# A fused attention and LoRA layer on one core: five transfers and sums moved at the start and near the end

## The chip, the core and the metric

The kernel runs on one core of a Trainium2 chip. The core has a matrix engine (TensorE, PE in the profile, with its weight loads as PEld), a vector engine (VectorE, DVE), a scalar engine (ScalarE, ACT), a general engine (GpSimd, POOL) and SyncE (SP), which here only issues transfers. Each engine runs its own list of instructions in order and waits for semaphores of the others. The metric is the device time of one execution in microseconds. A difference of 0.3% is about what a measurement of this kernel can tell from no change; here that is 2.45 us.

## The reference, cut to what matters

`x` is 2 x 512 tokens of 512 numbers, all in float32. There are 32 query heads, 8 key and value heads and a head size of 128.

```
q, k, v = x @ Wq + bq, x @ Wk + bk, x @ Wv + bv        # per head; q and k are then turned by the rope tables
p       = softmax(causal(q k^T / sqrt(128)))           # 4 query heads share one key head
x1      = layernorm(x + (p v) @ Wo + bo)
y       = x1 @ W_base^T + b_base + sum over 4 experts of alpha_e * 2 * (x1 A_e^T) B_e^T
out     = layernorm(x1 + y)                            # alpha: softmax over the 4 active experts' router logits
```

## The kernel before

**Units, parts, slots.** One unit `u` is a key head with one of the two sequences (16 units). A unit has four parts, one for each 128 queries; part `i` of a unit looks at `i + 1` tiles of 128 keys. All 64 parts stand in a list, and each takes four slots, one for each 32 queries of its four heads. Slot `T` computes the scores of step `T` on PE (L574); the other stages of the same step follow in later slots: masked maximum on DVE and exponential on ACT one slot later (L582, L589), reciprocal after two, normalisation on ACT after three (L597), transposition in 32 x 32 blocks on DVE after four (L605, L607). When the four steps of a part are transposed, `blocks_out` writes them to DRAM (`db`, four transfers, L615), and in a later slot `blocks_in` reads them back as `pT` with keys on the partitions (L626). From slot 4p + 12 on, one key tile in each slot, `weigh` multiplies `pT` by the values (L633). The scores have two PSUM buffers: the product of slot T can start only when the exponential of slot T - 2 has been taken.

The order is written out by hand. `slot(T)` issues, in this order, the projections of later units, the output products (`wo_products`), the scores, the weighting, the copies and the softmax stages; `put(T, f)` adds work at the end of a slot. The last two units are 14 and 15; their parts are 56 to 63, in the order of keys 1, 2, 3, 4 and then 3, 4, 1, 2 tiles. The parts that matter here are 58 (three tiles), 59 (four), 60 (three) and 61 (four).

**Strassen-like products.** The query projection and the output projection use seven products in place of eight, so sums of blocks are made ahead: `x_sums` on DVE (L441, four for each sequence), `w_sums` and `ctx_sums` on POOL (L449 to L452). Each result is added to `x_sb` from PSUM by `wo_adds` on DVE (L697). In most pairs of parts the add stands one slot after its product. For the last two pairs, 28 and 29, it stands in the same slot, and pair 28 begins in slot 247.

**The beginning.** SP loads four token tiles of x with the first key weights between them, then the query weights. PE transposes each tile, DVE or ACT copies it to `xT` (L288), and PE multiplies it by the key weights (L412). Then come the sums of x on DVE and the sums of query weights on POOL, which the seven products of the first query heads need.

**The end.** `W_base` has been transposed in blocks through DRAM (`wb_rows`) during the middle. From slot 237 on (`T_PROJ`) the memory of the projections is free, and `wb_sb` (1 MB in two transfers, L1231) lies in it. ACT copies it to `wbT` (L1226), which the first feed-forward products read in slot 251 (L805). Meanwhile DVE takes the statistics of the first four token tiles (L730), POOL does the Newton steps of their inverse roots (L754 to L757), and DVE centres them (L760).

**What orders one engine behind another here.** SP issues its transfers in program order: `pT` of a part waits there for all four `db` writes of that part to land. DVE's add waits for PE's product and holds everything that stands behind it on DVE.

Of the kernel before, what the change touches and what calls it, by code (L numbers as in the profile page):

```python
# [15 lines left out]
P = 128  # L16
# [3 lines left out]
D = 128  # L20
# [9 lines left out]
def postln_layer_kernel(  # L30
# [33 lines left out]
    nc = tc.nc  # L64
    B, S, HID = x.shape
    NT = B * S // P
    TPB = S // P
# [6 lines left out]
    NU = G * B  # L74
# [71 lines left out]
    wos = {}  # L146
    wvs = {}

    def load_k(g):
        wk_g = wts.tile([P, KC, D], F32, tag="wk_g", name=f"wk_{g}")  # L150
        nc.sync.dma_start(out=wk_g, in_=Wk[:, ts(g, D)].rearrange("(c p) n -> p c n", p=P))
        wqk["k", g] = wk_g

    def load_q(n, k):
# [15 lines left out]
    def load_x(t, n):  # L170
        nc.sync.dma_start(
            out=x_sb[:, t : t + n, :], in_=xf[t * P : (t + n) * P, :].rearrange("(t p) n -> p t n", p=P))


    for n in range(2):
# [6 lines left out]
        out=tri, in_=tri, pattern=[[-BLK, QB], [-1, BLK]], compare_op=ALU.is_ge,  # L182
# [7 lines left out]
    for z in zt:  # L190
        nc.gpsimd.memset(z, 0.0)

    for t in range(2):
        load_x(t, 1)
    load_k(0)
    for t in range(2, TPB):
        load_x(t, 1)
    load_q(0, 0)
    bqk = setup.tile([NBIAS, D], F32, name="bqk")
# [26 lines left out]

    ar_act = setup.tile([P, HID], F32, name="ar_act")
    lp_rep = setup.tile([P, P], F32, name="lp_rep")
    for part in (ar_act, lp_rep):
        nc.gpsimd.memset(part, 0.0)  # L230
    rb_act = setup.tile([EA, 1], F32, name="rb_act")
    pr_act = setup.tile([EA, 1], F32, name="pr_act")
    b_act = setup.tile([P, EA, BJ * RK], F32, name="b_act")
# [120 lines left out]
    parts = [(u, i) for u in range(NU) for i in ((2, 3, 0, 1) if u == NU - 1 else range(TPB))]  # L354
# [50 lines left out]
    def k_tile(u, t, c):  # L405

        g, b = unit(u)
        key = "k", u
        if t == c == 0:
            psq[key] = ps_k.tile([P, S], F32, tag="k", name="pp")  # L410
            in_psum.add(key)
        nc.tensor.matmul(  # L412
            psq[key][:, ts(t, P)], lhsT=wqk["k", g][:, c, :], rhs=xT[:, c, ts(b * TPB + t, P)],
            start=(t == c == 0), stop=(c == KC - 1), skip_group_check=True)
# [22 lines left out]
    def x_sums(b, step, engine=nc.vector):  # L437
        b11, b12, b21, b22 = (
            xT[:, CH * k : CH * (k + 1), b * S + a * TH : b * S + (a + 1) * TH] for k in range(2) for a in range(2))
        t1, t2, t3, t4 = (xs[:, b, k] for k in range(4))  # L440
        engine.tensor_tensor(  # L441
            *((t1, b12, b11), (t2, b22, t1), (t3, b22, b12), (t4, b21, t2))[step], ALU.subtract)

    def w_block(n, k, head, c_half):
        return wqk["q", n, k][:, CH * c_half : CH * (c_half + 1), ts(head, D)]

    def strassen_sums(engine, a11, a12, a21, a22, s1, s2, s4):

        engine.tensor_tensor(s1, a21, a22, ALU.add)  # L449
        engine.tensor_tensor(s2, s1, a11, ALU.subtract)  # L450
        engine.tensor_tensor(s4, a12, s2, ALU.subtract)
        engine.tensor_tensor(a21, a11, a21, ALU.subtract)  # L452

    def w_sums(n, k):
        w = ws[n, k] = proj.tile([P, 3, CH, D], F32, tag=f"ws{k}", name=f"ws_{n}_{k}")
        strassen_sums(
            nc.gpsimd, *(w_block(n, k, h, c) for h in range(2) for c in range(2)), *(w[:, m] for m in range(3)))
# [8 lines left out]
    def q_products(u, k, step):  # L466
        n, b = set_of(u), unit(u)[1]
        key = u, k
        w = ws[n, k]
        x1, x2 = (xT[:, CH * c : CH * (c + 1), ts(b, S)] for c in range(2))  # L470
        if step == 1:
            halves[key] = {"qx": ps_q.tile([P, TH], F32, tag="qx", name="qx")}
            product(halves[key]["qx"], w_block(n, k, 0, 0), x1[:, :, :TH], True)
        elif step == 2:
            halves[key]["qy"] = ps_q.tile([P, TH], F32, tag="qy", name="qy")
            product(halves[key]["qy"], w_block(n, k, 0, 1), x2[:, :, :TH], True)
        elif step == 6:
            product(halves[key]["qx"], w[:, 1], xs[:, b, 1], False)
        elif step == 5:
            product(halves[key]["qy"], w[:, 0], xs[:, b, 0], True)  # L480
        elif step == 7:
            product(halves[key]["qx"], w_block(n, k, 1, 0), xs[:, b, 2], False)
        elif step == 4:
            product(halves[key]["qx"], w_block(n, k, 1, 1), xs[:, b, 3], False)
        else:
            product(halves[key]["qy"], w[:, 2], x2[:, :, TH:], False)
# [6 lines left out]
    def q_copy(u, k, name):  # L493
        if name == "p1":
            psq["q", u, 2 * k] = proj.tile([P, S], F32, tag="raw0", name="q0", bufs=2)
        elif name == "u3":
            psq["q", u, 2 * k + 1] = proj.tile([P, S], F32, tag="raw1", name="q1")
        nc.scalar.copy(q_half(u, k, name), halves[u, k]["qx"])  # L498

    def q_sum(u, k, name):  # L500
        into = q_half(u, k, name)
        nc.vector.tensor_tensor(into, halves[u, k]["qy"], into, ALU.add)
# [106 lines left out]
    def blocks_out(p):  # L609

        i = parts[p][1]
        z, last = zt[i % 2], TPB - 2 + i % 2
        db[p] = dram.tile([QB, BLK, R, (i + 1) * P], F32, tag=f"db{i}", name=f"db_{p}")
        for r in range(R):
            nc.sync.dma_start(  # L615
                out=db[p][:, :, r, :].rearrange("q t x -> t q x"),
                in_=z[ts(r, BLK), :, last - i : last + 1].rearrange("t q j n s -> t q (j n s)"))

    def blocks_in(p):

        i = parts[p][1]
        pT[p] = work.tile([P, R, (TPB - 1 + i % 2) * P], F32, tag=f"pT{i % 2}", name=f"pT_{p}", bufs=1)

        for lo, hi in ((0, 1), (1, i + 1)) if i > 1 and parts[p][0] >= NU - 2 else ((0, i + 1),):
            cols = slice(lo * P, hi * P)
            nc.sync.dma_start(out=pT[p][:, :, cols], in_=db[p][:, :, :, cols].rearrange("q t r x -> (q t) r x"))  # L626

# [274 lines left out]
    def put(slot, f):  # L902
        extra.setdefault(slot, []).append(f)
# [95 lines left out]
        for step in (0, 1, 2, 3, 4, 6, 7):  # L999
            wo_at[8 * k + LAG_WO + step] = (k, (step,))  # L1000
    LAST_PAIRS = LAST + LAG_WO + 2
    for n, steps in enumerate(((0,), (1,), (2,), (3,), (4,), (6, 7))):
        wo_at[LAST_PAIRS + n] = (WO_PAIRS - 2, steps)
    for n, steps in enumerate(((0, 1), (2, 3), (4, 7), (6,))):
        wo_at[LAST_PAIRS + 6 + n] = (WO_PAIRS - 1, steps)
# [111 lines left out]
    for t in range(TPB - 2, TPB):  # L1117
        for c in range(KC):
            k_tile(0, t, c)
    for n in range(4):  # L1120
        x_sums(0, n)
    for k in range(2):
        w_sums(0, k)


    def v_first(t):
# [3 lines left out]
    for k in range(2):  # L1130
        for step in (1, 2, 6, 5, 7):
            q_products(0, k, step)
            if step == 1:
                q_copy(0, k, "p1")
            elif step == 2:
                q_sum(0, k, "p1")
                if k:
                    q_rope(0, 0, 2)
                    for part in range(3):
                        k_rope(0, part)  # L1140
                    for n in range(3):
                        x_sums(1, n, nc.gpsimd)
            elif step == 6:
                q_copy(0, k, "u2")
            elif step == 7:
                q_copy(0, k, "u3")
        q_sum(0, k, "u3")
        if k == 0:
            expert_rows()
        v_first(2 * k)  # L1150
        q_products(0, k, 4)
        q_copy(0, k, "c21")
        if k:
            prior_weights(0)
            q_rope(0, 3, 0)
        q_products(0, k, 3)
        q_sum(0, k, "u2")
        v_first(2 * k + 1)
        if k == 0:
            for t in range(TPB, NT):  # L1160
                transpose_token_tile(
                    xT[:, :, ts(t, P)], x_sb[:, t, :], *spare[(2, 3, 0, 3)[t - TPB]], nc.scalar.copy)
        for part in range(k, 3):
            q_rope(0, 2 * k + 1, part)
        if k:
            x_sums(1, 3, nc.gpsimd)
            for part in range(3):
                put(T_BEGIN + part, lambda part=part: q_rope(0, 2, part))
        else:
            for part in range(2):  # L1170
                q_rope(0, 0, part)
# [8 lines left out]
    T_PROJ = T_END - 19  # L1180
# [44 lines left out]
    def transposed_base(c):  # L1225
        nc.scalar.copy(  # L1226
            wbT[:, :, c // 2, ts(c % 2, P)].rearrange("p k (a s) -> p k a s", s=BLK),
            wb_sb[:, c].rearrange("p a k s -> p k a s"))

    for n in range(2):  # L1230
        put(T_PROJ + 9, lambda n=n: nc.sync.dma_start(  # L1231
            out=wb_sb[:, 2 * n : 2 * n + 2].rearrange("p c a k s -> p c a (k s)"),
            in_=wb_rows[:, :, 2 * n : 2 * n + 2].rearrange("q t c a x -> (q t) c a x")))
    for c in range(OC):
        put(T_PROJ + (12, 12, 13, 13)[c], lambda c=c: transposed_base(c))
    put(A - 5, lambda: f0[0].norm1.newton(0, 2))
    for k, f in enumerate(f0):
        put(A + (-7, -6, 0, 0)[k], f.stats)
# [160 lines left out]
```

## Time and profile before

| what | us |
|---|---|
| median of 3 runs (lowest, highest) | 815.27 (814.25, 816.87) |
| the profiled execution's own time | 816.12 |
| its span, first to last instruction | 814.3 |
| PE busy in it | 803.9 |
| DVE, ACT, POOL busy in it | 615.6, 382.6, 349.3 |
| granted TensorE clock | 0.999 of full speed |

The span is 1.8 us shorter than the profiled execution's own time; that execution is 0.85 us above the median of the runs. In the timeline, a row gives the start, the duration, the engine, the line, the operation with its output and inputs, and in brackets the idle time of the engine before it with what ended that. The rows of PE overlap by some tenths, because matmuls are pipelined and their ends are modelled.

### The profile page before, as it was taken

Reading aid. Unit: us, or ns where it says so; the run is one execution under the profiler, and the core shown is the slowest. Engines: PE = TensorE matmul, PEld = TensorE weight load, DVE = VectorE, ACT = ScalarE, POOL = GpSimd, SP = SyncE. Lnnn points to the kernel's source line nnn. Section 1 sums busy time; section 2 is a strip of 40 time slices with the busy share of each in tenths; the row PEclk is TensorE's granted clock in tenths of the full one; section 3 lists DMA queues with packets and bytes.
Section 4 is the critical chain, followed back from the end, with each engine's and each line's share of the span. In section 5 each row is a group of like instructions: output and inputs, shape, how many; then the busy total and the mean of one; then the engine's idle time right before and its main releaser. Section 6 shows DMA issues by size and latency. Waiting matters only on the chain.

```text
span 814.3 us, 11458 instructions
## 1 busy us (share of the span) xinstructions
PE 803.9 (99%) x3457; PEld 611.7 (75%) x3457; DVE 615.6 (76%) x1994; ACT 382.6 (47%) x1072; POOL 349.3 (43%) x404
## 2 busy tenths in 40 slices
PE   8999999999999999999999999999999999999997
PEld 7887777777777778777777878777777877657565
DVE  4778877687879886787868777787888689985455
ACT  2355454444545454545535454444545444654243
POOL 8666645421444445322443245343564433461033
PEclk9999999999999999999999999999999999999999
DMA  9025737355465647364554537355453725577311
GB/s 308 17 72 143 219 81 203 93 130 155 145 182 130 191 103 221 91 170 140 141 168 130 171 82 236 110 155 181 130 155 91 232 66 152 177 226 230 121 39 65
DMA packets 91376, 119.15 MB, mean 146 GB/s; under 512 B 6957, under 2 KB 71325, under 8 KB 89522
## 3 DMA queue, kind: packets, MB, share of 16 engines
q1 hardware_dynamic: 90642, 118.12, 50.4%
q8 instruction: 27, 0.44, 0.2%
q0 software_dynamic: 448, 0.14, 0.1%
q14 instruction: 35, 0.29, 0.1%
q10 hardware_dynamic: 224, 0.16, 0.1%
HBM read 72.78 MB, written 45.61 MB: 145 GB/s over the span
## 4 chain that ended last, share of the span: by engine, by line
PE 94%; POOL 2%; DVE 1%; DMA 1%; ACT 1%; issue 0%; DVEq 0%; POOLq 0%
PE pc L633 16%; PE sc L574 14%; PE qx L462 14%; PE wx L462 12%; PE qy L462 10%; PE wy L462 9%; PE kx L462 4%; PE vx L540 4%; PE py L805 3%; PE pv L360 3%; PE po L711 2%; PE pp L377 1%; DMA wb_sb<-wb_rows 1%; PE py L846 1%; PE tp L287 0%; PE ph L863 0%
## 5 line engine op out<-in xcount | busy, mean ns | idle before, releaser
L589 ACT ACTIVATE p<-sc,nmax 128x288 f32<-128x288 f32 (+15 forms) x256 | 124.2, 485 | 199.7 <-DVE nmax L582 181.2
L582 DVE CUSTOM_DVE_ANT_0 sc<-sc,maskw 128x288 f32<-128x288 f32 (+15 forms) x256 | 114.1, 446 | 131.7 <-PE sc L574 130.2
L633 PE MATMUL pc<-pT,v 128*128 128x512 f32 x320 | 165.6, 600 | 1.7 <-DMA pT<-db 1.6
L398 POOL TENSOR_TENSOR qT<-q,t 128x512 f32<-128x512 f32 x64 | 88.1, 1377 | 176.4 <-DVE q L397 165.3
L574 PE MATMUL sc<-kT,qT 128*128 128x160 f32 (+15 forms) x512 | 161.9, 398 | 0.9 <-ACT p L589 0.8
L597 ACT ACTIVATE p<-p,den 128x288 f32<-128x288 f32 (+15 forms) x256 | 133.2, 520 | 3.7 <-DVE den L593 3.7
L574 PEld LDWEIGHTS sc<-kT,qT 128*128 128x128 f32 x512 | 95.9, 190 | 20.1 <-issue 5.3
L449 POOL TENSOR_TENSOR cs<-ctxT 128x256 f32<-128x256 f32 x30 | 23.9, 796 | 168.6 <-PE wy L462 105.5
L640 ACT ACTIVATE ctxT<-pc,bqkT 128x512 f32<-128x512 f32 x64 | 44.0, 688 | 109.1 <-PE pc L633 108.5
L605 DVE STREAM_TRANSPOSE zt<-p 128x128 f32<-128x128 f32 (+2 forms) x192 | 81.6, 425 | 0.0
L633 PEld LDWEIGHTS pc<-pT,v 128*128 128x128 f32 x320 | 57.0, 190 | 21.2 <-issue 5.5
L498 ACT COPY q<-qx 128x256 f32<-128x256 f32 x128 | 47.4, 370 | 52.5 <-PE qx L462 52.3
L462 PE MATMUL qx<-xs,wq 128*128 128x256 f32 x256 | 66.2, 381 | 0.0
L462 PEld LDWEIGHTS qx<-xs,wq 128*128 128x128 f32 x256 | 47.4, 190 | 23.0 <-issue 18.7
L462 PE MATMUL wx<-wo,ctxT 128*128 128x256 f32 x240 | 61.7, 379 | 0.0
L607 DVE STREAM_TRANSPOSE zt<-p 128x32 f32<-128x32 f32 (+3 forms) x256 | 57.5, 225 | 0.0
L390 DVE SCALAR_TENSOR_TENSOR t<-q,bqkT,rope_sb 64x512 f32<-64x512 f32 x64 | 52.3, 818 | 3.5 <-ACT q L498 1.7
L697 DVE TENSOR_TENSOR x_sb<-wx,x_sb 128x256 f32<-128x256 f32 x120 | 50.4, 420 | 5.6 <-PE wx L462 5.6
L462 PEld LDWEIGHTS wx<-wo,ctxT 128*128 128x128 f32 x240 | 45.4, 190 | 9.3 <-issue 2.5
L393 DVE SCALAR_TENSOR_TENSOR t<-q,bqkT,rope_sb 64x512 f32<-64x512 f32 x64 | 50.3, 786 | 1.5
L589 ACT ACTIVATION_READ_ACCUMULATOR p<-sc,nmax 128x1 f32 x256 | 49.7, 194 | 0.0
L397 DVE SCALAR_TENSOR_TENSOR q<-q,bqkT,rope_sb 128x512 f32<-128x512 f32 x64 | 48.0, 751 | 0.1
(244 smaller groups left out, 1468.4 us busy)
## 6 DMA issues: line engine op xcount, KB each, us to landing
db<-zt SPq DMA_DIRECT2D x64, 256.0 KB, 3.9
pT<-db SPq DMA_DIRECT2D x14, 1024.0 KB, 4.8
db<-zt SPq DMA_DIRECT2D x64, 192.0 KB, 3.2
pT<-db SPq DMA_DIRECT2D x16, 768.0 KB, 4.4
wq<-in_L_attn_Wq_dram SPq DMA_DIRECT2D x20, 512.0 KB, 5.3
wo<-in_L_attn_Wo_dram SPq DMA_DIRECT2D x10, 1024.0 KB, 7.8
pT<-db SPq DMA_DIRECT2D x18, 512.0 KB, 4.2
db<-zt SPq DMA_DIRECT2D x64, 128.0 KB, 2.4
```

The lines of the kernel that those rows point to most:

```text
L390: nc.vector.scalar_tensor_tensor(t2[lo, :], q[hi, :], b_ap[hi, :], rope_sb[hi, 1, :], ALU.add, ALU.mult)
L393: nc.vector.scalar_tensor_tensor(t2[hi, :], q[lo, :], b_ap[lo, :], rope_sb[lo, 1, :], ALU.add, ALU.mult)
L398: nc.gpsimd.tensor_tensor(dst, t1[:, :].rearrange("p (n s) -> p n s", s=BLK), t2[:, :].rearrange("p (n s) -> p n s", s=BLK), ALU.add)
L462: nc.tensor.matmul(ps, lhsT=wt[:, c, :], rhs=xt[:, c, :], start=start and c == 0, stop=c == CH - 1, skip_group_check=True)
L574: nc.tensor.matmul(sc[s][:, :w], lhsT=qT[u][:, i * QB + n].rearrange("p r s -> p (r s)"), rhs=kT[u][:].rearrange("p n s -> p (n s)")[:, :w ...
L582: nc.vector.tensor_tensor_reduce(sc[s][:, :w], sc[s][:, :w], maskw[:, S - w :], -SCALE, -MASKED, ALU.add, ALU.min, nmax[s])
L589: nc.scalar.activation(ptile[s][:, :w], sc[s][:, :w], AF.Exp, bias=nmax[s], scale=-1.0, accum_out=rden[s])
L597: nc.scalar.activation(ptile[s][:, :w], ptile[s][:, :w], AF.Copy, scale=rden[s])
L605: nc.vector.transpose(z[:, :, last - i : last, n, :].rearrange("p q j s -> p j q s"), ptile[s][:, : i * P])
L607: nc.vector.transpose(z[:, : n + 1, last, n, :], ptile[s][:, i * P : w])
L633: nc.tensor.matmul(psc[p], lhsT=v_sb[g // VG, b][:, j, ts(g % VG, D)], rhs=pT[p][:, :, ts(j, P)], start=(j == 0), stop=(j == i))
L697: nc.vector.tensor_tensor(into, pw[k, bank], into, ALU.add)
```

## The change

- **Key weights.** The first key weights are issued by ScalarE, as its first transfer. SP issues the four tiles of x without a gap and then the query weights.
- **Fourth sum of x.** `x_sums(0, 3)` on DVE now stands behind the first sum of the query products. The two clears of `ar_act` and `lp_rep` on POOL now stand behind the sums of the query weights.
- **W_base.** The read-back of `wb_sb` moves from slot 246 to slot 237, and ACT's four copies from slots 249, 249, 250, 250 to slots 245, 246, 247, 248.
- **Long parts.** For the parts 58 to 61, the second and fourth of the four `db` writes are issued by ScalarE. Parts 58 and 60 are read back in one transfer where they were read in two (the first key tile, then the rest); parts 59 and 61 keep the two.
- **Two products.** The first two products of pair 28 move from slots 247 and 248 to slots 245 and 246, and their adds on DVE with them.

```diff
-    def load_k(g):
+    def load_k(g, queue=nc.sync):
         wk_g = wts.tile([P, KC, D], F32, tag="wk_g", name=f"wk_{g}")
-        nc.sync.dma_start(out=wk_g, in_=Wk[:, ts(g, D)].rearrange("(c p) n -> p c n", p=P))
+        queue.dma_start(out=wk_g, in_=Wk[:, ts(g, D)].rearrange("(c p) n -> p c n", p=P))
...
-    for t in range(2):
-        load_x(t, 1)
-    load_k(0)
-    for t in range(2, TPB):
+    load_k(0, nc.scalar)
+    for t in range(TPB):
         load_x(t, 1)
     load_q(0, 0)
...
-    for part in (ar_act, lp_rep):
-        nc.gpsimd.memset(part, 0.0)
...
+        late_part = i > 1 and parts[p][0] >= NU - 2
         for r in range(R):
-            nc.sync.dma_start(
+            (nc.scalar if late_part and r % 2 else nc.sync).dma_start(
...
-        for lo, hi in ((0, 1), (1, i + 1)) if i > 1 and parts[p][0] >= NU - 2 else ((0, i + 1),):
+        for lo, hi in ((0, 1), (1, i + 1)) if i == TPB - 1 and parts[p][0] >= NU - 2 else ((0, i + 1),):
...
-    for n, steps in enumerate(((0,), (1,), (2,), (3,), (4,), (6, 7))):
+    for n, steps in ((-2, (0,)), (-1, (1,)), (2, (2,)), (3, (3,)), (4, (4,)), (5, (6, 7))):
         wo_at[LAST_PAIRS + n] = (WO_PAIRS - 2, steps)
...
-    for n in range(4):
+    for n in range(3):
         x_sums(0, n)
     for k in range(2):
         w_sums(0, k)
+    for part in (ar_act, lp_rep):
+        nc.gpsimd.memset(part, 0.0)
...
                 q_sum(0, k, "p1")
-                if k:
+                if k == 0:
+                    x_sums(0, 3)
+                else:
...
-        put(T_PROJ + 9, lambda n=n: nc.sync.dma_start(
+        put(T_PROJ, lambda n=n: nc.sync.dma_start(
...
-        put(T_PROJ + (12, 12, 13, 13)[c], lambda c=c: transposed_base(c))
+        put(T_PROJ + 8 + c, lambda c=c: transposed_base(c))
```

## The prediction

> **What bounds the kernel now.** I read the page first (busy shares, the DMA row), then the waits, then PE's timeline where it shows idle time, and last what the other engines do beside those places.
>
> ```profile
> PE 803.9 (99%) x3457; PEld 611.7 (75%) x3457; DVE 615.6 (76%) x1994; ACT 382.6 (47%) x1072; POOL 349.3 (43%) x404
> PE pc L633 <- DMA pT<-db: 1.6, 2, 0.9
> PE sc L574 <- ACT p L589: 0.8, 1, 0.8
> PE qx L462 <- POOL ws L450: 0.7, 1, 0.7
> ```
>
> PE is idle for 814.3 - 803.9 = 10.4 us. The timeline places it: 1.2 before its first instruction, 5.3 behind its last (808.96 to the end), 0.35 at 5.13 (copy of the first tile), and four waits:
>
> ```profile
> 13.01 1.13 PE L462 MATMUL qx<-xs,ws 128*128 128x256 f32 x4 [0.70 <-POOL ws L450]
> ...
> 720.91 1.12 PE L633 MATMUL pc<-pT,v 128*128 128x512 f32 x2 [0.85 <-DMA pT<-db]
> ...
> 730.56 1.12 PE L633 MATMUL pc<-pT,v 128*128 128x512 f32 x2 [0.79 <-DMA pT<-db]
> ...
> 735.32 0.49 PE L574 MATMUL sc<-kT,qT 128*128 128x128 f32 x2 [0.82 <-ACT p L589]
> ```
>
> From 13 to 713 us nothing is idle, so what is won at the start is kept to slot 240. The four waits are 3.16 us, and with the 0.35 this is all that the change can reach: 3.5 us or 0.43%.
>
> The three late waits begin with these rows of SP, ACT and DVE:
>
> ```profile
> 709.74 2.21 SPq L615 DMA_DIRECT2D db<-zt  x4
> 714.67 1.20 SPq L626 DMA_DIRECT2D pT<-db  x2
> 724.81 1.02 SPq L1231 DMA_DIRECT2D wb_sb<-wb_rows  x2
> 736.57 1.21 SPq L626 DMA_DIRECT2D pT<-db  x2
> 733.21 1.14 ACT L1226 COPY wbT<-wb_sb 128x512 f32<-128x512 f32 x2 [2.10 <-DMA wb_sb<-wb_rows]
> ```
>
> wb_sb takes 8.4 us to land, holds ACT for 2.1 us and so delays the exponential that PE waits for at 735.32; it also shares the engines with part 59's pT (wait at 730.56).
>
> But PE is not alone there. DVE works nearly without a break from 706 to 731:
>
> ```profile
> core 0: us, PE busy (x) PEld busy (x) DVE busy (x) ACT busy (x) POOL busy (x), PEclk, DMA share, GB/s
> 706.00:731.00 25.00, 23.05 (x81) 13.69 (x80) 23.72 (x92) 16.27 (x41) 18.05 (x52) 1.00 0.67 188
> 731.00:741.00 10.00, 9.18 (x38) 6.53 (x37) 5.17 (x19) 5.13 (x17) 0.61 (x1) 1.00 0.64 212
> ```
>
> The reader should see 23.72 of 25 us: PE's stall at 720.91 lies beside a DVE that is itself 2 us behind (statistics and Newton of slot 245, 719.88 to 722.2). The score of slot 249 (729.34) is released by the exponential of slot 247, which DVE's maximum at 727.73 releases. Up to there DVE sets the pace, not PE.
>
> **The start, part by part.** POOL:
>
> ```profile
> 9.79 0.55 POOL L230 MEMSET ar_act<- 128x512 f32 x1
> 10.25 0.22 POOL L230 MEMSET lp_rep<- 128x128 f32 x1
> 10.56 1.26 POOL L449 TENSOR_TENSOR ws<-wq 128x256 f32<-128x256 f32 x1
> 11.90 1.05 POOL L450 TENSOR_TENSOR ws<-ws,wq 128x256 f32<-128x256 f32 x1
> ```
>
> With the clears behind, L449 starts at 9.8 instead of 10.56 and L450 ends at 12.2 instead of 12.95, before PE is through with qy (12.31): -0.70. The clears' new place costs nothing: POOL then waits 0.34 us for DVE before its first gather. The fourth x sum is first read by the product at 17.43, so its move costs nothing either; q_sum, which it freed, is bound by qy (12.31).
>
> Key weights. Before, issued at 1.67, landed after 3.6 us (5.27), just under the copy that PE waits for (5.43). Now they are issued at 0.73 on ScalarE's queue. By that landing time alone they arrive at 4.3 and PE loses nothing. The Trainium skill speaks against that ("DMA: Bandwidth & Descriptors", Queues, rings and completion order): each DMA engine takes turns between queues that have work, a packet at a time. The weights are 512 rows of 512 B and the four x tiles 512 rows of 2 KB; turn by turn, the weights end with the fourth tile, which lands at 2.7 + 4.5 = 7.2, and PE's first key product moves from 5.48 to 7.2, +1.7. The nearest rows of a second queue beside SP's stream are GpSimd's small transfers, 5.5 us from issue to landing. I take 0.73 + 5.5 = 6.2: +0.75. Products behind it follow without a gap and POOL's sums are then in time. Sum of the start: -0.70 + 0.75 = +0.05, with ends -0.7 and +1.0.
>
> **The end, part by part.** wb_sb in slot 237: SP waits for the last query rope on POOL (L398, 706.00 to 707.27), issues at 707.3 and 707.8, and reaches part 58's db at 709.74 in time. Moving data from 708.2 at the 370 to 400 GB/s of the best slices, 1 MB ends at 711. The db data began at 710.5, so db58 lands about 0.5 later.
>
> Two queues for db: the four issues take 2.21 us on SP; half of them would save 1.1 us if issue were the bound. The trace has the engines 90% busy or more from 711 to 714 at about 230 GB/s, and the skill's same page (Issuing engines are not separate DMA queues) says that a second issuing engine saves issue time only. By issue, pT58 leaves 1.1 earlier; by the rule, not at all. I take nothing, so pT58 is issued at 714.67 + 0.5 = 715.2.
>
> One read for part 58: the undivided 768 KB reads of the middle land after 4.2 to 4.5 us: 719.4. The divided one delivered its first tile in 3.2 (717.9, PE wanted it at 718.28) and the rest at 720.8. So PE now waits in slot 244 for s = 719.4 - 718.28 = 1.1 us, in place of 0.85 one slot later.
>
> The new wait. In slot 245 DVE's add for the moved product stands ahead of transposes, statistics, Newton and all later maxima; PE's product stands behind the waiting pT58. It ends at 718.28 + s + 0.86 + 1.03 = 720.2 + s. DVE is there at 719.34 (behind the add at 719.00) and now waits 0.86 + s; before it was already late when this add came (724.71). With the add itself, 0.34, DVE's chain is later by 1.2 + s: Newton, POOL's steps, the maximum of slot 247: 727.73 + 2.3 = 730.0. Then maximum and read 0.75, exponential 0.7, score of slot 249 at 731.6 instead of 729.34. Here pT59 has landed (no wb_sb beside it), so 0.79 is gone. ACT then has the last copy of wbT (0.57), two copies of x1T (1.0), a normalisation (0.7) and the next exponential (0.3): the score of slot 250 comes at 734.1 and that of slot 251 at 734.1 + 0.19 + 0.86 + 0.86 = 736.0. The 0.82 is gone too, but before it stood at 735.32: +0.7. For s = 0 the same sum gives -0.4.
>
> ScalarE's issues: two of 0.42 to 0.57 each in slots 239, 243, 247 and 251, behind DVE's transposes. Behind them stand a normalisation, needed two slots later, and the next exponential. In slot 239 it moves from 711.19 to 711.4, in 243 from 717.58 to 718.4 while its score is wanted at 721; in 247 ACT is ready at 730.1, before DVE. Nothing, with an upper end of 1.7 for an issue (one of SP's took that at 718): then slot 247 loses up to 1.5. The missing second issues of pT58 and pT60 free SP for 0.6 each, where nothing waits.
>
> Sum: +0.05 + 0.7 = +0.75 us. Span 814.3 to 815.05; the profiled execution 816.87; on the median of the runs 815.27 + 0.75 = 816.0.
>
> **The rivals.** (1) Slower. The read-back again takes the 8.4 us of its row, now ahead of db58: 707.3 + 8.4 = 715.7. What was queued behind it at 725.87 landed after 8.7 to 9.2 us where 3.3 was usual. Then db58 lands near 716.5, pT58 near 721.3, s = 3.0 instead of 1.1, and the end loses 0.7 + 1.9 = 2.6; with +0.05 at the start 817.9. It decides from a landing of pT58 after 721.1. For: the same megabyte on the same queue. Against: its 8.4 us were shared with pT59 and db60, 2.8 MB in 9 us, and at 708 and 709 the engines are idle.
>
> (2) Faster. All four waits go and DVE catches up: -3.16, 812.1. For: every one has its edit. Against: it needs pT58 before 718.3 and DVE not to wait in slot 245, where its order says that it does.
>
> (3) The start alone is lost or won: 815.3 to 817.0 with the end as above; inside the forecast.
>
> **How the numbers follow.** Forecast 0.60, its own range 814.2 to 817.6 (ends of the start -0.7 and +1.0, s from 0 to 1.8, noise of the median). Rival 1: 0.28. Rival 2: 0.12. What a measurement can tell here is 0.3%, 2.45 us, so faster means below 812.8 and slower above 817.7. Rival 2 gives 0.10 of faster and 0.02 of same; rival 1 gives 0.23 slower, 0.05 same; the forecast 0.04 slower, 0.56 same. Faster 0.10, same 0.63, slower 0.27. The range 813.5 to 819.2 leaves out most of rival 2 and the tail of rival 1.
>
> **What would show it.** Right: no wait of qx on ws L450; a wait of the first kx-type product (L412) for wk of about 0.75; a DVE wait of x_sb on wx near 720 of about 2 us; pc in slot 244 waiting about 1.1 for pT; no ACT wait for wb_sb; the score of slot 249 waiting for ACT. Wrong: pT58 landing before 718.3 or after 721; wb_sb landing after 713; DVE idle before slot 249.

## The result, and the profile after

The changed kernel takes 817.92 us (median of 12 runs, 816.94 to 818.77), the kernel before 816.03 us (12 runs, 814.25 to 817.1). The ratio is 1.0023 with a 95% interval of 1.0015 to 1.0032: 1.9 us slower, 1.2 to 2.6 by the interval. That is less than the 0.3% named above, but the interval keeps clear of 1. The forecast of +0.75 had the sign and, on 815.27, lay 1.9 below the time; part of that gap is the median before, which more runs moved from 815.27 to 816.03. The profiled execution after has a span of 816.3 us (before 814.3).

First PE's busy line on the page of the kernel after, then the waits of PE: engine, line, what waited, whom for, total, times, longest. The changed kernel's lines have numbers 3 or 4 lower than before (574 became 570, 633 became 630, 462 became 458).

```profile
PE 805.0 (99%) x3457; PEld 611.9 (75%) x3457; DVE 617.4 (76%) x1994; ACT 382.2 (47%) x1072; POOL 348.5 (43%) x404
PE sc L570 <- ACT p L585: 2.1, 3, 1.3
PE pc L630 <- DMA pT<-db: 1.2, 1, 1.2
PE pv L356 <- DMA wv<-in_L_attn_Wv_dram: 0.4, 1, 0.4
PE tp L283 <- DMA x_sb<-_attn_hidden_states_dram: 0.4, 1, 0.4
```

The wait of qx for ws is gone, one of the two waits for pT is gone. In their place stand three waits of scores for ACT (2.1 in all, before 0.8 in one) and two small ones at the start. PE's timeline places them:

```profile
5.41 1.11 PE L283 MATMUL tp<-ident,x_sb 128*128 128x128 f32 x4 [0.37 <-DMA x_sb<-_attn_hidden_states_dram]
...
16.23 1.99 PE L356 MATMUL pv<-wv,xT 128*128 128x256 f32 x8 [0.37 <-DMA wv<-in_L_attn_Wv_dram]
...
720.35 1.12 PE L630 MATMUL pc<-pT,v 128*128 128x512 f32 x2 [1.19 <-DMA pT<-db]
...
727.01 1.13 PE L570 MATMUL sc<-kT,qT 128*128 128x512 f32 x2 [0.54 <-ACT p L585]
729.41 0.41 PE L570 MATMUL sc<-kT,qT 128*128 128x32 f32 x2 [1.27 <-ACT p L585]
...
732.78 0.43 PE L570 MATMUL sc<-kT,qT 128*128 128x64 f32 x2 [0.29 <-ACT p L585]
...
737.17 0.38 PE L570 MATMUL sc<-kT,qT 128*128 128x128 f32 x2
```

The wait of the end's chain begins on DVE, in slot 245:

```profile
722.38 0.42 DVE L694 TENSOR_TENSOR x_sb<-wx,x_sb 128x256 f32<-128x256 f32 x1 [2.24 <-PE wx L458]
```

This is the add of the moved product. Before, DVE ran on at 719.34; now it stands still for 2.24 us, to 722.38, until PE, held in slot 244 for the undivided part 58, has made the product. The table by stretch shows it as a share:

```profile
706.00:731.00 25.00, 21.77 (x72) 12.31 (x71) 21.16 (x79) 15.89 (x39) 16.02 (x50) 1.00 0.70 219
731.00:741.00 10.00, 9.58 (x43) 6.71 (x42) 6.73 (x28) 6.17 (x19) 2.72 (x3) 1.00 0.73 234
```

The columns are PE, PEld, DVE, ACT, POOL, clock, DMA share, GB/s. In the first stretch DVE is busy for 21.16 us where it was 23.72, and PE for 21.77 instead of 23.05. Both have lost time there, and the second stretch is fuller because it holds what was pushed out.

**A ruler.** Landing times of transfers differ from one execution to the next, so whole spans of single profiles are poor evidence. Three marks on PE split a profile instead: the score of slot 237 (448 columns) shows what the start did; from there to the score of slot 249 (64 columns) shows DVE's chain; from there to slot 251 (128 columns) shows the landings of part 59 and of W_base. What comes behind slot 251 lasts 78.6 to 79.1 us in twelve of the fourteen profiles and 80.0 in two, so in these two the marks leave out about 1 us (below, two queues alone).

| kernel | slot 237 at | 237 to 249 | 249 to 251 |
|---|---|---|---|
| before | 704.91 | 24.43 | 5.98 |
| after | 705.64 | 27.14 | 4.39 |

So this pair of profiles holds +0.73 of the start, +2.71 of DVE's chain and -1.59 behind it: 1.85.

The issues of SP at the end, of the kernel after (start, duration, queue, line):

```profile
708.01 0.82 SPq L1232 DMA_DIRECT2D wb_sb<-wb_rows  x2
710.46 0.80 SPq L612 DMA_DIRECT2D db<-zt  x2
715.97 0.34 SPq L623 DMA_DIRECT2D pT<-db  x1
...
734.35 0.34 SPq L623 DMA_DIRECT2D pT<-db  x1
```

ACT's rows, its own issues among them, and from the DMA view the row of W_base (transfers, KB of each, median us from issue to landing):

```profile
710.46 0.85 ACTq L612 DMA_DIRECT2D db<-zt  x2
720.51 0.61 ACT L1227 COPY wbT<-wb_sb 128x512 f32<-128x512 f32 x1
```

```profile
wb_sb<-wb_rows SPq DMA_DIRECT2D x2, 512.0 KB, 4.7
```

SP issues two of four db writes in 0.80 us instead of four in 2.21, ScalarE the other two beside it, yet part 58's pT is issued 5.51 us after the first db write (before 4.93). The copy of wbT has no bracket: W_base, issued at 708.01, landed 4.2 us (first half) and 5.1 us (second) after its issue, long before ACT asked at 720.51. The wait of 2.10 us is gone. Part 60's pT is issued at 734.35, 2.2 us sooner than before (736.57), in a kernel that is later at that place.

### The profile page after: what moved, and what is told of

Read it like the earlier page. It is cut to its first block, busy times and chain, and to the rows that moved or that the text cites. A ratio compares the mean times of both kernels' runs of the same rounds, so it can differ in the third digit from the quotient of the medians.

```text
span 816.3 us, 11458 instructions
## 1 busy us (share of the span) xinstructions
PE 805.0 (99%) x3457; PEld 611.9 (75%) x3457; DVE 617.4 (76%) x1994; ACT 382.2 (47%) x1072; POOL 348.5 (43%) x404
## 4 chain that ended last, share of the span: by engine, by line
PE 94%; DMA 3%; DVE 1%; ACT 0%; POOL 0%; issue 0%; SPq 0%; ACTq 0%; DVEq 0%; POOLq 0%
PE pc L630 16%; PE sc L570 14%; PE qx L458 13%; PE wx L458 12%; PE qy L458 10%; PE wy L458 9%; PE kx L458 4%; PE vx L536 4%; PE py L802 3%; PE pv L356 3%; PE po L708 2%; PE pp L373 1%; DMA wv<-in_L_attn_Wv_dram 1%; DMA pT<-db 1%; PE py L843 1%; DMA db<-zt 1%
```

## The experiments

Changes against "after" undo a part; changes against "before" do one part alone. All ratios are to the kernel before on the same chip. A ratio need not be the quotient of the two medians: with two queues alone the medians are 0.85 us apart and the ratio is 1.0001. "Marks" are the three numbers of the table above.

**Undo the key weights' move** (after, but Wk again on SP behind the second x tile; the other starting edits stay).

```diff
-    load_k(0, nc.scalar)
-    for t in range(TPB):
-        load_x(t, 1)
+    for t in range(2):
+        load_x(t, 1)
+    load_k(0)
+    for t in range(2, TPB):
+        load_x(t, 1)
```

> The changed kernel with the first key weights back on SyncE behind the second tile of x; all else as changed. My theory: at the start the changed kernel loses because its query weights wait on SyncE for the key weights to land (issue at 4.66 instead of 3.22), which makes the value weights late (0.63 us of PE). Put back, that is gone, and the clears that were moved away still bring 0.70: first value product at 15.0, score of slot 237 at 704.2 (before 704.91, changed 705.64). The end stays as in the changed kernel, 1.0 to 1.1 later than before counted from slot 237. Sum against before: -0.7 + 1.1 = +0.4 us. Rival: the late value weights come from the traffic of the start as a whole (the same bytes in another order); then the value product still waits and the score of slot 237 stays near 705.

Measured: 817.15 us, ratio 1.0015 (1.0007 to 1.0024). The marks are 705.39, 27.04 and 4.39. The end is that of after to a tenth, so nothing of it comes from the key weights. The time is about 0.65 better than the change's 1.0023, but the two intervals overlap. The expected start did not come: slot 237 at 705.39 instead of 704.2, the first value product at 16.24 instead of 15.0. In the profile PE waits 0.29 at the third x tile instead of 0.37 at the second.

**Undo the two products** (after, but the products of pair 28 again in slots 247 and 248).

```diff
-    for n, steps in ((-2, (0,)), (-1, (1,)), (2, (2,)), (3, (3,)), (4, (4,)), (5, (6, 7))):
+    for n, steps in enumerate(((0,), (1,), (2,), (3,), (4,), (6, 7))):
```

> The changed kernel with the first two products of pair 28 back in slots 247 and 248, their adds with them. My theory: the end loses because DVE waits 2.2 us in slot 245 for a product that stands behind the late keys of part 58, and everything on DVE up to the score of slot 249 is later. Without it DVE does not wait (under 0.3 us), the score of slot 249 comes about 24.4 us after that of slot 237 as before (changed 27.1), those of slots 250 and 251 without the old waits: the score of slot 251 about 1 us earlier than before counted from slot 237, 2 us earlier than in the changed kernel. Against before: +0.7 at the start, -1 at the end: -0.3 us. Rival: the end loses because the keys of part 58 are late in themselves (1.2 us wait of PE in slot 244); then the score of slot 251 gains under 0.5 against the changed kernel.

Measured: 815.04 us, ratio 0.9986 (0.9978 to 0.9995), 3.0 us better than the change and just faster than before. Marks: 704.13, 24.64, 4.17. PE still waits for part 58 in slot 244, as long as ever, and it no longer matters:

```profile
718.99 1.13 PE L630 MATMUL pc<-pT,v 128*128 128x512 f32 x2 [1.34 <-DMA pT<-db]
...
728.77 0.33 PE L570 MATMUL sc<-kT,qT 128*128 128x64 f32 x2
```

```profile
724.29 0.42 DVE L694 TENSOR_TENSOR x_sb<-wx,x_sb 128x256 f32<-128x256 f32 x1 [0.24 <-PE wx L458]
```

The score of slot 249 has no bracket, and DVE's longest wait for the moved product is 0.24. PE's stall of 1.34 lies beside a DVE that works on; in these kernels the stall costs where DVE's next instruction needs the product behind it.

**Undo both.** The two edits above together.

```diff
-    load_k(0, nc.scalar)
-    for t in range(TPB):
+    for t in range(2):
+        load_x(t, 1)
+    load_k(0)
+    for t in range(2, TPB):
...
-    for n, steps in ((-2, (0,)), (-1, (1,)), (2, (2,)), (3, (3,)), (4, (4,)), (5, (6, 7))):
+    for n, steps in enumerate(((0,), (1,), (2,), (3,), (4,), (6, 7))):
```

> The changed kernel with both undone: key weights on SyncE behind the second tile of x, and the two products back in slots 247 and 248. My theory: the two losses are separate and add up: start -0.7, end -1, sum -1.7 us against before (ratio near 0.998). Rival: PE earlier at the start only meets the late keys of part 58 or DVE sooner, and the gain of the start is lost at the end: within 0.5 us of before.

Measured: 814.40 us, ratio 0.998 (0.997 to 0.9991), the lowest of all. Marks: 704.91, 24.70, 4.12. Its distance from the version just above (0.0006) is within the intervals.

**Query bias ahead of the key weights** (after, with the small transfer bqk issued first on ScalarE). In the changed kernel, SP issues the query weights at 4.66 where it did at 3.22 before, and the waits of SP's queue name the key weights' landing (last column the longest):

```profile
SPq L157 <- DMA wk<-in_L_attn_Wk_dram: 2.1, 1, 2.1
```

Counted by the time of issue on SP and ScalarE, the query weights are the ninth transfer and the key weights among the first; before, the small query bias was among the first. What fits is that the program lets its transfers signal their end on eight semaphores in turn, so that the ninth waits for the first; the semaphores themselves stand in no trace.

```diff
+    bqk = setup.tile([NBIAS, D], F32, name="bqk")
+    nc.scalar.dma_start(out=bqk[:H, :], in_=bq.rearrange("(h d) -> h d", d=D))
     load_k(0, nc.scalar)
...
-    bqk = setup.tile([NBIAS, D], F32, name="bqk")
-    nc.scalar.dma_start(out=bqk[:H, :], in_=bq.rearrange("(h d) -> h d", d=D))
```

> The changed kernel with one order turned: ScalarE issues the query bias (16 KB) ahead of the key weights. Then the transfer that the query weights wait for on SyncE is the bias and no longer the key weights. My theory: query weights issued at about 3.2 instead of 4.66, value weights in time, first value product at 15.5 to 15.7 without a wait, score of slot 237 at 705.0 (changed 705.64). The second tile of x stays late (PE waits for it near 5.4). Rival: the hold is no cause, the second queue's sharing is; then the value product still waits about 0.4 to 0.8 for its weights.

Measured in one execution: 817.17 us; marks 704.60, 27.30, 4.40. The query weights, ninth, wait for the query bias and are issued at 3.20. The hold moves on: the second query weights, eleventh, wait 1.2 us for the key weights, by issue now the third, and are issued at 5.34. In both orders the held transfer stands eight behind the one it waits for, as eight semaphores in turn would have it. PE waits neither for the value weights nor, against what was expected, for the second x tile. Whether the hold costs time is asked below.

**The start alone** (before, with the start's edits only).

```diff
...
+    load_k(0, nc.scalar)
+    for t in range(TPB):
         load_x(t, 1)
...
-    for part in (ar_act, lp_rep):
-        nc.gpsimd.memset(part, 0.0)
...
-    for n in range(4):
+    for n in range(3):
         x_sums(0, n)
...
+                if k == 0:
+                    x_sums(0, 3)
...
```

> The kernel before with the start of the change alone (key weights first and on ScalarE's queue, the two clears and the fourth x sum later). The end is as before, so its time against before is the start's share. Theory of this study (the key weights' transfer holds the issue of the query weights, so value weights and second x tile come late): between 0 and +0.8 us, 816.0 to 817.2. The prediction's +0.05: no difference. A start that gains, -0.7: 815.6. In the profile the score of slot 237 stands at 704.9 +- 0.7.

Measured: 815.24 us against 815.48, ratio 0.9991 (0.9982 to 1.0001). Marks: 704.78, 24.43, 4.03. In its profile the query weights come late as in after (4.61), and still pv has no wait. The only gap is the 0.36 us before the second x tile. The last mark is the surprise: the end of this kernel is that of before, yet the wait of 0.79 for part 59 is not there, and ACT's wait for W_base is

```profile
731.14 1.14 ACT L1226 COPY wbT<-wb_sb 128x512 f32<-128x512 f32 x2 [0.16 <-DMA wb_sb<-wb_rows]
```

instead of 2.10. The five kernels that read W_base at slot 246 had 2.10, 0.16, 1.18, 0.60 and 0.49 there (before, start, products, queues, products with undivided reads). The row that the prediction built on was the largest of five.

**W_base alone** (before, with the read-back at slot 237 and the copies in slots 245 to 248).

```diff
-        put(T_PROJ + 9, lambda n=n: nc.sync.dma_start(
+        put(T_PROJ, lambda n=n: nc.sync.dma_start(
...
-        put(T_PROJ + (12, 12, 13, 13)[c], lambda c=c: transposed_base(c))
+        put(T_PROJ + 8 + c, lambda c=c: transposed_base(c))
```

> The kernel before with W_base read back at slot 237 and its copies in slots 245 to 248, nothing else. Theory: this is the part that gains. ACT's wait of 2.10 for wb_sb, PE's wait of 0.82 behind it and of 0.79 for part 59 go; part 58's db starts about 0.5 later, its first tile still lands by about 718.4; from the score of slot 237 to that of slot 251 about 29.0 instead of 30.41; -1.4 us, 815.0, ratio 0.9983. Rival (the read-back delays part 58 by several us and PE waits in slot 244 for it): 30.4 or more, no gain.

Measured: 814.87 us, ratio 0.9989 (0.9978 to 0.9999). Marks: 705.30, 24.83, 4.00. The last mark loses the 2 us that the profile of before had, the middle one gains 0.4, because part 58 comes later:

```profile
721.82 1.12 PE L633 MATMUL pc<-pT,v 128*128 128x512 f32 x2 [1.32 <-DMA pT<-db]
```

That is 0.85 before. First db issue to pT issue is 710.12 to 715.56, 5.44 us with one queue. By the ratio the edit is worth 0.9 us (0.1 to 1.8); the expected 1.4 and the 1.6 of the two waits lie within that interval. The rival (30.4 or more from slot 237 to slot 251, no gain) did not happen: it is 28.83.

**The two products alone** (before, with them in slots 245 and 246).

```diff
-    for n, steps in enumerate(((0,), (1,), (2,), (3,), (4,), (6, 7))):
+    for n, steps in ((-2, (0,)), (-1, (1,)), (2, (2,)), (3, (3,)), (4, (4,)), (5, (6, 7))):
```

> The kernel before with the two products moved to slots 244 and 245, nothing else. Theory (DVE's add waits in slot 245 for PE's product and everything behind it on DVE is late): DVE waits 0.9 to 1.8 us for wx near 720, the score of slot 249 waits for ACT's exponential, from the score of slot 237 to that of slot 251 30.8 to 32.2 instead of 30.41; +0.4 to +1.8 us. Rival (the wait needs the late, undivided part 58): no long wait of DVE, within 0.3 us of before.

The edit puts them in slots 245 and 246; the slots in the expectation are one too low.

Measured: 815.61 us against 815.48, ratio 0.9994 (0.9983 to 1.0004). Marks: 705.80, 25.68, 5.06.

```profile
721.08 0.42 DVE L697 TENSOR_TENSOR x_sb<-wx,x_sb 128x256 f32<-128x256 f32 x1 [0.79 <-PE wx L462]
```

```profile
731.48 0.43 PE L574 MATMUL sc<-kT,qT 128*128 128x64 f32 x2 [0.20 <-ACT p L589]
```

With the divided read DVE waits for the moved product too, but only 0.79, and its chain is 1.25 later than before. The profile shows a cost, the ratio does not: the expected +0.4 to +1.8 us did not come. Behind the chain, ACT comes to the copies of W_base later as well and waits less for it (1.18 instead of 2.10), so part of the delay may fall into a wait that was there anyway; in all the profile has 30.74 from slot 237 to slot 251 where before had 30.41. But this profiled execution took 817.14 us, 1.5 above the median of its kernel, and the waits for W_base differ between executions, so this reading is argued and not shown. The rival said no long wait of DVE; there is one, at a price that the ratio does not show.

**Two queues alone** (before, with the second and fourth db write of the long parts on ScalarE).

```diff
+        late_part = i > 1 and parts[p][0] >= NU - 2
-            nc.sync.dma_start(
+            (nc.scalar if late_part and r % 2 else nc.sync).dma_start(
                 out=db[p]
```

> The kernel before with the writes of db for the long parts 57 to 60 issued alternately by SP and ScalarE, reads divided as before. If the issue of four transfers by one engine (2.21 us) set the landing of db, part 58's pT is issued 1.1 us sooner after the first db issue (3.8 instead of 4.93) and the wait of pc in slot 245 falls or goes. If the data rate sets it, 4.9 stays and the time is that of before. ScalarE's issues in its stream could cost up to 0.5 us.

The edit takes the parts 58 to 61; here too the expectation's count is one too low.

Measured: 816.33 us against 815.48, ratio 1.0001 (0.9988 to 1.0014). Marks: 705.41, 24.41, 4.48.

```profile
710.23 0.79 SPq L616 DMA_DIRECT2D db<-zt  x2
715.21 1.20 SPq L627 DMA_DIRECT2D pT<-db  x2
```

From the first db issue to pT's issue it is 4.98 us (before 4.93). Issue is not what bounds it, and by the ratio the time stays as it was, within 1.1 us. The value with W_base ahead is the same for one queue (5.44) and two (5.51): the 0.5 us there come from the megabyte ahead, not from the queues. Here W_base, read late, has a second price that the marks do not cover. PE waits for part 60 behind slot 251:

```profile
740.49 1.10 PE L634 MATMUL pc<-pT,v 128*128 128x512 f32 x2 [1.00 <-DMA pT<-db]
```

Of the five kernels with the late read of W_base, this one and the one with products and undivided reads (0.61) have this wait; of the nine with the early read, none has.

**Products and undivided reads** (before, with both).

```diff
-        for lo, hi in ((0, 1), (1, i + 1)) if i > 1 and parts[p][0] >= NU - 2 else ((0, i + 1),):
+        for lo, hi in ((0, 1), (1, i + 1)) if i == TPB - 1 and parts[p][0] >= NU - 2 else ((0, i + 1),):
```

> The kernel before with the two products sooner and the parts 58 and 60 read undivided, nothing else of the change. Theory (the products cost through DVE's add in slot 245, and their price grows with PE's wait for the undivided part 58 in slot 244): pc of slot 244 waits 0.9 to 1.3, DVE waits about 2 us for wx instead of the 0.79 with the products alone, three scores wait for ACT, from the score of slot 237 to that of slot 251 31.2 to 32 us; 817.0 to 817.9, ratio 1.001 to 1.0025. Rival (the early read-back of W_base is what makes the products dear): time as with the products alone, ratio 0.9994.

Measured: 817.14 us, ratio 1.0014 (1.0006 to 1.0021). Marks: 705.21, 26.61, 4.37.

```profile
719.40 1.13 PE L633 MATMUL pc<-pT,v 128*128 128x512 f32 x2 [0.68 <-DMA pT<-db]
```

```profile
721.43 0.42 DVE L697 TENSOR_TENSOR x_sb<-wx,x_sb 128x256 f32<-128x256 f32 x1 [1.73 <-PE wx L462]
```

W_base is read late here, nothing lies ahead of part 58, and PE's wait in slot 244 is 0.68 instead of 1.19; DVE's follows, 1.73 instead of 2.24. From the products alone (0.9994) to this (1.0014) only the read has changed. The undivided reads without the moved products were not run on the kernel before; with W_base early they cost nothing (below), so it is the two edits together that cost. The ratio came as expected, the distance (30.98) a little short of the 31.2 expected, and some of the time lies behind it (0.61 of wait for part 60). The rival said that the products are dear only with the early read of W_base. They cost without it, so it is out as the only cause; with it, DVE's wait is 0.5 longer.

**After with divided reads** (the whole change except the undivided reads).

```diff
-        for lo, hi in ((0, 1), (1, i + 1)) if i == TPB - 1 and parts[p][0] >= NU - 2 else ((0, i + 1),):
+        for lo, hi in ((0, 1), (1, i + 1)) if i > 1 and parts[p][0] >= NU - 2 else ((0, i + 1),):
```

> The changed kernel with part 58 and 60 read divided as before, the rest of the change kept. Theory: part 58's first tile lands in time for slot 244, the wait of 1.19 there goes, DVE waits about 0.8 for wx instead of 2.24, from the score of slot 237 to that of slot 251 about 29.9 instead of 31.53; ratio to before 0.999 to 1.0005 instead of 1.0023. Rival: 1.0023 stays, since the first tile is late anyway behind the earlier read-back.

Measured: 815.9 us against 815.85, ratio 1.0 (0.999 to 1.0009). Marks: 704.13, 25.91, 5.36.

```profile
719.65 0.42 DVE L694 TENSOR_TENSOR x_sb<-wx,x_sb 128x256 f32<-128x256 f32 x1 [1.01 <-PE wx L458]
```

```profile
731.63 1.13 PE L630 MATMUL pc<-pT,v 128*128 128x512 f32 x2 [1.15 <-DMA pT<-db]
```

The other half of the same test: with the products sooner and W_base early, the divided read alone takes DVE's wait from 2.24 to 1.01, the middle mark from 27.14 to 25.91, and the loss against before is gone. The time came as expected; the distance from slot 237 to 251 (31.27) did not, because PE waited 1.15 for part 59 in this execution.

**After without the moved products, and with the bias first; the same with divided reads** (the second has the edit of the version before this as well).

```diff
...
+    nc.scalar.dma_start(out=bqk[:H, :], in_=bq.rearrange("(h d) -> h d", d=D))
     load_k(0, nc.scalar)
...
-    for n, steps in ((-2, (0,)), (-1, (1,)), (2, (2,)), (3, (3,)), (4, (4,)), (5, (6, 7))):
+    for n, steps in enumerate(((0,), (1,), (2,), (3,), (4,), (6, 7))):
```

> The changed kernel with the two products back in slots 247 and 248 and the small query-bias transfer ahead of the key weights on ScalarE's queue, so that the query weights' issue waits for a transfer that lands early. Against the version with the products back alone (ratio 0.9986): theory, no wait of PE for value weights or second x tile at the start, a further -0.3 to -0.7 us, ratio 0.998. Rival (the start decides nothing that can be measured): 0.9986 again.

> As the kernel just before this one, with parts 58 and 60 read divided as well: start, early W_base, two queues and later products. Theory: without the moved products DVE has slack behind slot 244, so PE's wait of 1.3 there is only exchanged for one in slot 245; the score of slot 249 stays released by ACT behind DVE; ratio 0.998 as there, within 0.3 us. Rival: -0.5 to -1.0 more, 0.997.

Measured: 815.27 us, 0.999 (0.9984 to 0.9997), and 815.44 us, 0.9997 (0.9988 to 1.0005). Marks: 704.60, 24.50, 5.54 and 704.23, 24.53, 5.96. Neither is better than the version with the later products alone (0.9986): the bias ahead of the key weights takes PE's last wait out of the start and gains nothing that shows. In both, PE waited for part 59 (1.42 and 1.84). Why part 59 comes in time in some executions and not in others wasn't settled.

With W_base early, all four pairs of the two edits were run:

| ratio to before | divided reads | undivided reads |
|---|---|---|
| products late | 0.9997 (bias first) | 0.9986; 0.999 (bias first) |
| products sooner | 1.0 | 1.0023 |

The products with divided reads, or undivided reads with late products, cost nothing that shows; the two together stand 0.0023 to 0.0037, about 1.9 to 3.0 us, above the other cells.

**All marks together**, in groups by what stands in slot 245 and how part 58 is read:

| products, reads | kernels | 237 to 249 |
|---|---|---|
| late | before, start alone, W_base alone, queues alone, and the four with the products put back | 24.41 to 24.83 |
| sooner, divided | products alone, after with divided reads | 25.68, 25.91 |
| sooner, undivided | products and undivided, key weights back, after, bias first | 26.61, 27.04, 27.14, 27.30 |

The groups do not touch. Their means are 24.6, 25.8 and 27.0: 1.2 us for the products and 1.2 more where part 58 is read undivided, whatever the start, the queues and W_base do.

## Why the prediction was right in sign and short in size

**The start: +0.05 in the sum; sign open, size under 1 us.** The step that failed is the key weights' landing at 6.2. They were there at 4.66, when SP's held issue came free. What was late was the second x tile, which now moves beside the key weights of another queue: PE's transposes wait for it until 5.41, and the first key product stands at 6.31 instead of 5.48, +0.83 where +0.75 was said. The size was met by luck, for another reason. First the row before, then the row after:

```profile
5.48 1.16 PE L412 MATMUL pp<-xT,wk 128*128 128x128 f32 x8 [0.35 <-DVE xT L288]
```

```profile
6.31 1.29 PE L408 MATMUL pp<-xT,wk 128*128 128x128 f32 x8
```

The prediction's reading of the turn-taking rule of the Trainium skill ("DMA: Bandwidth & Descriptors", Queues, rings and completion order), that equal numbers of rows end together, would have had the key product at 7.2. The weights were there well before that, so the reading did not hold here; whether the rule itself does, no run shows.

The wait of pv for the value weights, 0.37, was not foreseen: SP's issue of them stood behind the held query weights. But the same late issue cost nothing in three other executions of this start.

The profile before was itself no usual case, and the sum rested on it. Its key weights landed 3.6 us after their issue; in the six other profiles with the key weights on SP it was 4.1 to 4.9. In the four other kernels with the unchanged start, the first key product waits for them and stands at 6.15 to 6.55, where the four profiles with the whole new start have 5.92 to 6.31. In these four POOL's sums are in time, so the wait of qx for ws, which the clears were to save, is not there. In its place PE waits 0.46 to 0.63 before qy, for a sum on DVE that stands behind the fourth sum of x. PE and DVE of W_base alone, which has the unchanged start:

```profile
6.32 1.24 PE L412 MATMUL pp<-xT,wk 128*128 128x128 f32 x8 [0.50 <-DMA wk<-in_L_attn_Wk_dram]
...
14.55 1.13 PE L462 MATMUL qy<-xs,ws 128*128 128x256 f32 x4 [0.46 <-DVE q L502]
```

```profile
12.96 1.21 DVE L441 TENSOR_TENSOR xs<-xT,xs 128x512 f32<-128x512 f32 x1
14.09 0.41 DVE L502 TENSOR_TENSOR q<-qy,q 128x256 f32<-128x256 f32 x1
```

And DVE of the kernel after, where the two stand in the other order:

```profile
13.37 0.42 DVE L498 TENSOR_TENSOR q<-qy,q 128x256 f32<-128x256 f32 x1 [0.31 <-PE qy L458]
13.71 1.17 DVE L437 TENSOR_TENSOR xs<-xT,xs 128x512 f32<-128x512 f32 x1
```

None of the nine kernels with the sum moved has this wait. So the move that the prediction put at nothing removes a wait that four of the five profiles of the old start have, and the -0.70 of the clears belonged to the one execution that it read. The third block of products (qx<-xs,wq) starts at 14.20 to 14.96 in the four profiles with the whole new start, at 15.44 to 15.75 in these four of the old one, and at 14.84 in the profile before. No run moved the fourth sum alone.

Slot 237 stands at 705.28 in the mean of seven profiles with the key weights on SP (704.91 to 705.80), at 704.67 in four with the new order (704.13 to 705.64) and at 704.48 in three with the bias first. The ratios say -0.7 us for the start added to before, and +0.65 and +0.5 for the key weights' move kept in two versions of the end; none is clear of noise. So the +0.73 of the profile after is not a loss shown.

**The end: +0.7 in the sum, +1.12 in the pair of profiles, more by the ratios.** Step by step:

- *W_base lands by 711, not after 8.4 us.* Late by 1 to 2.5 us, without effect. Its halves landed 4.2 and 5.1 us after their issue, near 712.2 and 713.5; the second is past the 713 that was to show the forecast wrong, but ACT asked only at 720.51. Rival 1, which named just the time that came (817.9), hit it by luck; its mechanism did not happen.
- *db58 0.5 later, two queues worth nothing.* Right: from the first db issue to pT's issue it is 5.51 instead of 4.93, and 4.98 with the queues alone. The skill's rule that was weighed (the same page, Issuing engines are not separate DMA queues: a second engine saves issue time only) agrees with this row.
- *s = 1.1.* A little short. PE's product for part 58 starts 4.38 us after the issue (the sum had 4.2), at 720.35; less the start's 0.73 that is 1.34 behind the 718.28 of before. PE's idle time there is 1.19.
- *DVE waits about 2.0 and its chain is 2.3 later.* The mechanism was right, and undoing it gave the strongest effect of the study (3.0 us with the key weights on ScalarE, 2.9 with them on SP). The size was short by 0.4: DVE waited 2.24 and the score of slot 249 came 2.71 later.
- *The waits of 0.79 and 0.82 go: -1.6.* This is the term that was mis-sized most. In the pair of profiles it is exact (4.39 between the slots 249 and 251 where the sum had 4.4), but those two waits were landings that one execution happened to have. With the same end, the start alone had neither (4.03). W_base alone gained 0.9 by its ratio. With 2.7 from the marks for DVE's chain and 0.9 for W_base, the end would be +1.8, an estimate that with a start near nothing comes to the measured +1.9. The 0.9 is uncertain by as much again (0.1 to 1.8), so this closes the sum but does not prove it.

The profiled execution of before was ordinary in total (816.12 against a median of 816.03) because its start was among the better ones and its end among the worse.

The single effects add up to less: W_base alone is -0.9 us, products with undivided reads +1.1, queues 0, start -0.7 to +0.65, in sum -0.5 to +0.9. Each is uncertain by 0.6 to 1.1 us, the sum by about 1.7 (an estimate, from the four intervals), so the gap to the measured 1.9 (1.2 to 2.6) may be noise in part. It would also fit the products' delay and W_base's wait standing in the same microseconds: where DVE is late, ACT comes late to W_base too, and less is left to gain (0.49 of wait with products and undivided reads). This reading is argued from single profiles and not shown.

What was said to show the forecast right, then: the wait of qx is gone, DVE's wait near 720 is there, pc waits in slot 244, ACT does not wait for wb_sb, the score of slot 249 waits for ACT. Only the key product's wait for wk did not come: in the changed kernel the product waits for nothing, and in four kernels of the old start it waits for wk.

## What to carry to other kernels

A product moved sooner brings its consumer with it: if the consumer stands in order on an engine that sets the pace, everything behind it waits for whatever the product waits for. Ask of each earlier step what its engine would have done in that time, and make sure that the data ahead of it is early before moving it. And a landing that a single profile shows as a wait, or as in time, is one draw; look at it in a second kernel that shares the same stage before it is booked as a gain or as nothing.

## What the hardware showed that was not expected

The order of small transfers at the start decides which large one is held. With the key weights as ScalarE's first transfer, the ninth of SP and ScalarE together, the query weights, was issued at 4.66, 4.61, 4.80 and 4.47 in four executions; with the query bias first, at 3.20, 3.20 and 3.21, and the eleventh was held to 5.34, 5.30 and 5.16 instead. SP issues in order, so all transfers behind the held one come later, though they wait for nothing themselves. It cost PE no time that the ratios show.

```profile
3.20 0.38 SPq L157 DMA_DIRECT2D wq<-in_L_attn_Wq_dram  x1
3.62 0.50 SPq L201 DMA_DIRECT2D rope_sb<-in_rope_tables_dram  x1
5.30 0.38 SPq L157 DMA_DIRECT2D wq<-in_L_attn_Wq_dram  x1
```

These are SP's issues in the version with the bias first and the products late: 0.4 to 0.5 us apart, then a hold of 1.2 us, until the key weights have landed.
